# Attention in eight batches: six of seven products of y in blocks, seeded by copies within PSUM, with sums moved behind the last product and x1 added early

## The chip, the cores and the metric

The kernel runs on one core of a Trainium2 chip. A core has five engines, each with its own queue worked off in order: TensorE (PE in the profile; its weight loads are PEld), VectorE (DVE), ScalarE (ACT), GpSimd (POOL) and SyncE (SP, which only issues DMAs here). Engines wait for each other through semaphores. Matmul results go to PSUM, eight banks of 512 floats for each of 128 partitions; everything else lies in SBUF. The metric is device time in microseconds (us), as the median of three runs.

## The reference: what is computed

For each of 8 batches, with x1 (here `x`) and x2 (here `ctx_2048`) of 512 channels by 1024 positions, all in float32:

```python
q = jnp.einsum('bcn,dc->bnd', x1, Wq) + bq
k = jnp.einsum('bcn,dc->bdn', x2, Wk) + bk[:, None]
v = jnp.einsum('bcn,dc->bdn', x2, Wv) + bv[:, None]
attn = jax.nn.softmax(jnp.einsum('bnd,bdm->bnm', q, k), axis=2)
attn_out = jnp.einsum('bcm,bnm->bcn', v, attn)
return attn_out + x1
```

q and k have 64 rows. The kernel takes the value product in another order: first y = x2 times the transposed exponentials (512 x 1024 x 1024 per batch), divided by the sums of the exponentials, then Wv times y (512 x 512 x 1024), plus bv and x1.

## The kernel before, in words

Both large products are done by the Winograd form of Strassen's scheme: each matrix is cut into 2 x 2 blocks, and seven products of block sums take the place of eight. `MULT` names them 1, 2, 6, 7, 5, 3, 4, with a left and a right factor each: a11, a12, a21, a22 and the sums S1 to S4 on the left (x2, transposed, loaded as four blocks), t11 to t22 and T1 to T4 on the right (exponentials). Products 1, 6, 5, 3 add up in the two PSUM banks called a (a0, a1, one for each 128 rows of a block), products 2, 7, 4 in the banks c. A running sum is a state: ACT copies it out to SBUF (u1, u6, u5) where a later result needs it. The first stage gives the blocks y11, y12, y21, y22, the second (`second`) the output blocks in the same manner, with w in place of a and y in place of t.

A product of the first stage has two forms. The full one (`multiply`, L321) is 8 matmuls of 512 columns, two instructions each. The one in blocks applies the scheme once more inside (`inner_left`, `inner_right` make the sums on DVE, L355 and L367; `inner_product`, L374, the 7 small products, 14 matmuls of 256 columns, two instructions each). Its seven partial results pass through a bank called chain and one called third, both from the pool `sc`, which also serves the scores; ACT copies the chain's states to a tile d (L383), and DVE adds d afterwards (`complete`, L452, and the lines that follow: L462, L471, L483). `multiply_2` does the same for product 2 in a form of its own (L418).

The loop is over batches: `period(s, n, nn, nnn)` is written for batch s while the scores, maxima and exponentials of the next batch n and the queries and keys of the one after it (nn) are slipped in between. All orders are written by hand; each engine does its part of the program in the order of the text, and a waiting instruction holds up all that stand behind it on its engine. A column half h of a batch (0 or 1, 512 positions) has tiles e[h]; its scores are four pairs of matmuls, the third pair in a bank pair of the first stage (c for half 0, a for half 1), the others in `sc`. DVE takes maxima over the tiles (L211, L215), POOL an all-reduce over partitions (L221), DVE subtracts the maximum (L249), ACT takes the exponential (L253). Sums of exponentials go the same way (L226), by DVE for half 1 (`sums`), and for half 0 by accumulating DMAs of POOL (`add_tile`, L555). `shares` inverts them: a DMA gathers the row into 128 partitions, DVE inverts, and two DMAs through DRAM spread it again.

Which products are in blocks depends on the batch: products 3 and 4 in batch 0; 2, 3 and 4 in batches 1 and 6; 2, 7, 3 and 4 in batches 2 to 5 and 7 (`seven`). S1, S2, S3 of the next batch are DVE sums at the end of a period (`sum_a`, L110), S4 one behind product 2, T4 from batch 2 on a copy by ACT and an accumulating DMA (L278, L280). `evict_y` adds and scales the blocks of y (L502, L505, L507). `evict_o` adds the bias (L548 on DVE, L544 on ACT), lets POOL add x1 from DRAM by an accumulating DMA (L551) and SP store (L552). q lies twice in SBUF, at both halves of the partitions; ACT issues the two DMAs that double it (L167).

Of the kernel before, what the change touches and what calls it, by code (L numbers as in the profile page):

```python
# [15 lines left out]
def kernel(  # L16
# [48 lines left out]
    P = 128  # L65
# [35 lines left out]
    def left_sums(a, *ks):  # L101

        for k in ks:
            x, y, op = {
                "S1": ("21", "22", ALU.add),
                "S2": ("11", "S1", ALU.subtract),
                "S3": ("11", "21", ALU.subtract),
                "S4": ("12", "S2", ALU.add),
            }[k]
            nc.vector.tensor_tensor(a["21" if k == "S3" else k], a[x], a[y], op)  # L110
            if k == "S3":
                a["S3"] = a["21"]

    class Batch:
        def __init__(self, b):
            self.b = b
            self.a, self.e, self.t, self.y, self.o = {}, {}, {}, {}, {}
            self.mx, self.top, self.den, self.few, self.rden = {}, {}, {}, {}, {}
            self.tmp, self.bank = {}, {}
            self.inner = {}  # L120
# [19 lines left out]

    def project(s, nm, w_sb, bank=None):
# [16 lines left out]
    def queries(s):  # L158

        ps = project(s, "q", wq_sb)  # L160
        s.q = sb.tile([P, N], F32, tag="q", name=f"q_{s.b}", bufs=2)
        for h, r, o in ((0, lo, hi), (1, hi, lo)):
            nc.scalar.activation(
                s.q[r, ts(h, H)], ps[r, :], AF.Identity, bias=bq_sb[r, :]
            )
        for h, r, o in ((0, lo, hi), (1, hi, lo)):
            nc.scalar.dma_start(s.q[o, ts(h, H)], s.q[r, ts(h, H)])  # L167
# [64 lines left out]
    def shares(s, h):  # L232

        nc.vector.reciprocal(s.few[h], s.few[h])
        row = dram.tile([1, H], F32, tag="row", name=f"row_{s.b}_{h}")
        nc.gpsimd.dma_start(row.rearrange("o (p f) -> (o p) f", p=P), s.few[h])
        s.rden[h] = s.den[h]
        nc.gpsimd.dma_start(s.rden[h], row.broadcast_to([P, H]))
# [32 lines left out]
    def sum_t4(s):  # L271

        s.t["T4"] = t4 = sb.tile([P, MH, H], F32, tag="eT4", name=f"eT4_{s.b}")
        if s.b < 2:
# [7 lines left out]
    def sum_e(s, *ks):  # L282
        for i in (0, 2):
# [4 lines left out]
    def sum_y(s, k):  # L288
        if k == "T1":
            for n in ("T1", "T2", "T4"):  # L290
                s.y[n] = sb.tile([P, 2, H], F32, tag=f"y{n}", name=f"y{n}_{s.b}")
            s.y["T3"] = s.y["12"]
        right_sums(s.y, k)
# [14 lines left out]
    def multiply(s, stage, i, left, right, n_k, last=False, hook=None):  # L308
# [3 lines left out]
        ka, kb, bank, opens = MULT[i]  # L312
        for j in range(2):
# [21 lines left out]

    LEFT = (
        ("S1", "21", "22", ALU.add),
        ("S2", "11", "S1", ALU.subtract),
        ("S3", "11", "21", ALU.subtract),
        ("S4", "12", "S2", ALU.add),  # L340
    )
    RIGHT = (
        ("T1", "12", "11", ALU.subtract),
        ("T2", "T1", "22", ALU.subtract),
        ("T3", "22", "12", ALU.subtract),
        ("T4", "21", "T2", ALU.add),
    )

# [9 lines left out]
    def inner_right(s, i, x, *tags):  # L358
# [4 lines left out]
        shape = [P, 4 // len(tags), MH // 2, H // 2]  # L363
        sums = [sb.tile(shape, F32, tag=t, name=f"eI{i}{t}_{s.b}") for t in tags]
        for z, (k, x, y, op) in enumerate(RIGHT):
            v[k] = sums[z // shape[1]][:, z % shape[1]]
            nc.vector.tensor_tensor(v[k], v[x], v[y], op)  # L367
        s.inner[i, "t"] = v
# [16 lines left out]
    def inner_bank(s, i, z):  # L385
        return ps_s.tile([P, 2, H], F32, tag="sc", name=f"ps_i{i}{z}_{s.b}")[:, 0, left]

    def multiply_2(s):

        chain = ps_a.tile([P, H // 2], F32, tag="c0", name=f"ps_i20_{s.b}")  # L390
        second = ps_a.tile([P, H // 2], F32, tag="c1", name=f"ps_i21_{s.b}")
        third = inner_bank(s, 2, 2)
        uv = sb.tile([P, 4, H // 2], F32, tag="i2", name=f"i2_{s.b}")
        u, v = uv[:, 0:2], uv[:, 2:4]
        for z, ps, opens, *copies in (
            (1, chain, True, v[:, 0, :]),
            (2, second, True),
            (6, chain, False, u[:, 0, :]),
            (7, third, True, v[:, 1, :]),
            (5, chain, False, u[:, 1, :]),  # L400
            (4, third, False),
            (3, chain, False),
        ):
            inner_product(s, 2, z, ps, opens, *copies)

        def evict():

            u0, u1 = s.tmp[1][:, 0, :], s.tmp[1][:, 1, :]
            s.y["11"] = y = sb.tile([P, 2, H], F32, tag="y11", name=f"y11_{s.b}")
            for out, x, z in (  # L410
                (u0[:, left], u0[:, left], v[:, 0, :]),
                (y[:, 0, left], second, u0[:, left]),
                (u1, u1, u.rearrange("p a n -> p (a n)")),
                (y[:, 1, right], v[:, 1, :], u1[:, right]),
                (y[:, 1, left], third, u1[:, left]),
                (y[:, 0, right], chain, u0[:, right]),
            ):
                nc.vector.tensor_tensor(out, x, z, ALU.add)  # L418

        return evict  # L420

    def multiply_onto(s, i, d_tag, v_tag, hooks={}):
# [5 lines left out]
        bank, opens = MULT[i][2:]  # L428
        if opens:
            for j in range(2):  # L430
                s.bank[bank, j] = ps_a.tile([P, H], F32, tag=f"{bank}{j}", name=f"ps_y{bank}{j}_{s.b}_{i}")
        b0, b1 = (s.bank[bank, j] for j in range(2))
        chain, third = inner_bank(s, i, 0), inner_bank(s, i, 2)
# [503 lines left out]
```

## Time and profile before

| what | value |
|---|---|
| median of 3 runs | 691.22 us (691.01 to 691.45) |
| span of the profiled execution | 689.5 us |
| its own time | not listed apart from the three runs |
| granted TensorE clock over the span | 0.999 |
| batch 3, from the start of its product 1 to that of the next batch | 83.66 us |
| DMA moved | 109.05 MB, mean 158 GB/s |

The profile records one execution. A group of it has the kernel's line, the engine, the operation, what is written from what, and how often; then the busy time, the mean of one, and the idle time of the engine ahead of it with what ended it. Instructions of one engine overlap a little at their ends, so two in a row take less than the sum of their durations. Batches are told apart by the order of time: a period begins with product 1 of the first stage (8 matmuls into ps_ya from e and a).

### The profile page before, as it was taken

What the parts mean: (1) busy time and instruction counts of PE and PEld (TensorE: products, weight loads), DVE (VectorE), ACT (ScalarE), POOL (GpSimd) and SP (SyncE); (2) the same over time, 40 slices, a digit from 0 to 9 for tenths busy, and PEclk for the clock granted to TensorE, in tenths of its full rate; (3) what the DMA queues carried; (4) which work ended last, traced back from release to release, by engine and by line L of the source; (5) the groups of instructions that cost most, each with busy time, mean ns of one, the idle gap of its engine ahead of it and who ended that gap; (6) DMA issues with size and microseconds to landing.
All of it is one profiled execution on the core that took longest, in us unless ns stands there. A gap on an engine that the chain in (4) does not pass through costs nothing.

```text
span 689.5 us, 6656 instructions
## 1 busy us (share of the span) xinstructions
PE 683.1 (99%) x2252; PEld 365.3 (53%) x2252; DVE 630.4 (91%) x809; ACT 275.7 (40%) x439; POOL 189.3 (27%) x147
## 2 busy tenths in 40 slices
PE   9999999999999999999999999999999999999997
PEld 5333554535545465455654566454754545545763
DVE  1999999988999889998999989999899988999894
ACT  2734263146233562435533454324544245333220
POOL 0124113521423123231232321423223241324100
PEclk9999999999999999999999999999999999999999
DMA  9666266954558854696638867298642874259403
GB/s 301 263 218 231 70 183 120 252 162 92 184 106 208 236 100 160 129 243 182 125 130 160 241 176 166 69 187 224 181 81 41 185 200 77 62 108 248 102 0 123
DMA packets 44723, 109.05 MB, mean 158 GB/s; under 512 B 4880, under 2 KB 7184, under 8 KB 44688
## 3 DMA queue, kind: packets, MB, share of 16 engines
q0 software_dynamic: 17424, 36.25, 30.1%
q1 hardware_dynamic: 25856, 70.13, 29.4%
q10 hardware_dynamic: 1408, 2.23, 1.1%
q8 instruction: 18, 0.29, 0.2%
q14 instruction: 17, 0.14, 0.1%
HBM read 72.62 MB, written 16.81 MB: 130 GB/s over the span
## 4 chain that ended last, share of the span: by engine, by line
PE 94%; DMA 3%; SPq 1%; ACT 1%; DVE 1%; issue 0%; DVEq 0%
PE ps_ya L321 24%; PE ps_i L374 17%; PE ps_oa L321 16%; PE ps_oc L321 12%; PE ps_s L191 6%; PE ps_yc L374 5%; PE ps_q L149 4%; PE ps_k L149 3%; PE ps_ya L374 3%; PE ps_yc L321 3%; DMA a<-in_x2T_dram 1%; DMA x_in_x_dram<-in_x_dram 1%; DMA x_head<-in_x_dram 1%; PE ps_sc L191 1%; PE ps_sa L191 1%; DVE aS L110 0%
## 5 line engine op out<-in xcount | busy, mean ns | idle before, releaser
L321 PE MATMUL ps_ya<-eT,aS 128*128 128x512 f32 x256 | 113.1, 595 | 0.0
L332 ACT COPY uy<-ps_ya 128x512 f32<-128x512 f32 x48 | 28.0, 586 | 138.9 <-PE ps_ya L321 124.9
L321 PEld LDWEIGHTS ps_ya<-eT,aS 128*128 128x128 f32 x256 | 48.0, 190 | 60.9 <-issue 58.8
L253 ACT ACTIVATE e<-e 128x1024 f32<-128x1024 f32 x60 | 63.0, 1059 | 42.3 <-DVE e L249 40.8
L249 DVE TENSOR_TENSOR e<-e,top 128x1024 f32<-128x1024 f32 x60 | 69.8, 1214 | 11.0 <-POOL top L221 11.0
L221 POOL PARTITION_ALL_REDUCE top<-max x16 | 32.8, 2052 | 154.6 <-DVE max L215 79.3
L226 POOL PARTITION_ALL_REDUCE den<-sum x16 | 59.2, 3701 | 40.8 <-DVE sum L215 35.8
L321 PE MATMUL ps_oa<-yT,w_S 128*128 128x512 f32 x128 | 57.6, 593 | 0.0
L321 PE MATMUL ps_oc<-y,w 128*128 128x512 f32 x128 | 57.6, 593 | 0.0
L321 PE MATMUL ps_ya<-e,a 128*128 128x512 f32 x128 | 56.3, 593 | 0.3 <-ACT e L244 0.3
L200 ACT COPY e<-ps_s 128x1024 f32<-128x1024 f32 x46 | 45.7, 1028 | 19.3 <-PE ps_s L191 18.1
L332 ACT COPY uo<-ps_oa 128x512 f32<-128x512 f32 x48 | 27.4, 583 | 53.0 <-PE ps_oa L321 41.3
L383 ACT COPY d<-ps_i 128x256 f32<-128x256 f32 x84 | 29.3, 374 | 47.6 <-PE ps_i L374 47.0
L551 POOL DMA_DIRECT2D uo<-in_x_dram x21 | 24.9, 1184 | 85.0 <-DVE uo L548 85.0
L191 PE MATMUL ps_s<-q,k 64*128 64x512 f32 x188 | 47.3, 608 | 0.8 <-ACT q L590 0.8
L555 POOL DMA_DIRECT2D sum<-e x21 | 25.7, 1222 | 66.5 <-DMA sum<-e 32.7
L321 PEld LDWEIGHTS ps_ya<-e,a 128*128 128x128 f32 x128 | 24.2, 190 | 31.3 <-issue 29.6
L321 PEld LDWEIGHTS ps_oa<-yT,w_S 128*128 128x128 f32 x128 | 24.2, 190 | 30.8 <-issue 29.9
L321 PEld LDWEIGHTS ps_oc<-y,w 128*128 128x128 f32 x128 | 24.0, 190 | 31.0 <-issue 28.5
L211 DVE TENSOR_TENSOR max<-max,e 128x1024 f32<-128x1024 f32 x30 | 36.7, 1225 | 3.0
L507 DVE TENSOR_TENSOR y<-y,den 128x512 f32<-128x512 f32 x54 | 33.7, 681 | 0.0
L548 DVE SCALAR_TENSOR_TENSOR uo<-ps_oc,bv_sb,uo 128x512 f32<-128x512 f32 x42 | 29.5, 741 | 1.6 <-PE ps_oc L321 1.6
(142 smaller groups left out, 1274.5 us busy)
## 6 DMA issues: line engine op xcount, KB each, us to landing
x_in_x_dram<-in_x_dram SPq DMA_DIRECT2D x60, 512.0 KB, 6.2
a<-in_x2T_dram SPq DMA_DIRECT2D x32, 512.0 KB, 6.3
sum<-e POOLq DMA_DIRECT2D x21, 512.0 KB, 5.1
uo<-in_x_dram POOLq DMA_DIRECT2D x21, 512.0 KB, 6.4
out_dram<-uo SPq DMA_DIRECT2D x21, 512.0 KB, 4.1
eT<-eT POOLq DMA_DIRECT2D x12, 512.0 KB, 6.8
den<-row POOLq DMA_DIRECT2D x16, 256.0 KB, 3.6
r<-in_x_dram POOLq DMA_DIRECT2D x7, 512.0 KB, 8.7
```

The costliest lines, as they stand in the source:

```text
L149: nc.tensor.matmul(ps[r, :], w_sb[:, c, :], s.x[:, c, ts(h, H)], start=(c == 0), stop=(c == CT - 1),)
L191: nc.tensor.matmul(ps[g], s.k[r, ts(i, P)], s.q[r, ts(h, H)], start=True, stop=True)
L200: nc.scalar.copy(e[:, :, i, :], whole)
L211: nc.vector.tensor_tensor(f, e[:, :, 0, :] if i == 1 else f, e[:, :, i, :], op)
L221: nc.gpsimd.partition_all_reduce(s.top[h], s.mx[h][:, 0, :], P, ReduceOp.max)
L226: nc.gpsimd.partition_all_reduce(s.den[h], s.mx[h][:, 0, :], P, ReduceOp.add)
L249: nc.vector.tensor_tensor(e, e, top, ALU.subtract)
L253: nc.scalar.activation(e, e, AF.Exp)
L321: nc.tensor.matmul(ps[:, n], left[ka][:, k, ts(j, P)], right[kb][:, k, n], start=opens and k == 0, stop=i in (2, 3, 4) and k == n_k - 1, s ...
L332: nc.scalar.copy(s.tmp[i][:, j, :], ps)
L374: nc.tensor.matmul(ps, s.inner[i][ka][:, k, :], s.inner[i, "t"][kb][:, k, :], start=opens and k == 0, stop=z in (2, 3, 4) and k == MH // 2 ...
L507: nc.vector.tensor_tensor(y[:, j, :], y[:, j, :], rden, ALU.mult)
```

## The change

In batches 1 to 7 (the second batch on) products 1 and 2, 7, 3 and 4 are in blocks, and in batches 1 to 5 product 5 as well; 6 stays full. Batch 0 keeps 3 and 4.

`multiply_seeded` takes the place of the block form for 1, 2, 7 and 3. Its two result banks are new, and are begun not by a matmul but by ACT copies of the chain's states, from one PSUM bank into another; the small products 2, 4 and 3 then add onto what was copied. DVE's `complete` adds the one remaining piece v into the second bank, in place. Products 5 and 4 keep the tile d. Product 3 no longer adds onto the state of bank a: with signs turned in S4 and in the sums of w, y22 - y12 comes out directly as T3 (`evict_t3`), and y12 is never made. Product 7's banks are copied out for it by ACT (`copy_7`).

Work that moves: S1 of the next batch is loaded and summed by two DMAs (`begin_s1`, `end_s1`), S2 and S3 are made by an ACT negation and an accumulating DMA (`negate`, `add_11`), T3 of the first stage likewise (`sum_t3`; by DVE in batches 0 and 7), T4 by copy and DMA from batch 1 on. The total of half 0's exponentials is joined behind the last output product of the period before, its inverse and the spreading of it stand apart (`invert`, `spread`). Right-hand sums T1 and T3 are one instruction. The scaling of y11, T3 and y22 is one instruction each, behind the scores of half 1. The second stage's product 1 opens two banks of `sc` (p), is copied by ACT into bank a, and product 2 adds onto p; block 11's output then goes by ACT. x1 is added to block 21's state ahead of its last product (`add_x1`). The DMAs that double q are issued by SP; the queries of a batch use bank c0, and are taken out in the middle of product 5 (`evict_q`).

The core of the diff, helpers first:

```diff
+            if k == "S3":
+                nc.vector.tensor_tensor(a["21"], a["11"], a["21"], ALU.subtract)
+                a["S3"] = a["21"]
+            elif k == "S4":
+                nc.vector.scalar_tensor_tensor(a[k], a["12"], -1.0, a["S2"], ALU.mult, ALU.subtract)
+            else:
+                x, y, op = {"S1": ("21", "22", ALU.add), "S2": ("11", "S1", ALU.subtract)}[k]
+                nc.vector.tensor_tensor(a[k], a[x], a[y], op)
...
+    def begin_s1(s):
+        s.a["S1"] = sb.tile([P, MH, C // 2], F32, tag="aS1", name=f"aS1_{s.b}")
+        nc.sync.dma_start(s.a["S1"], x2T[s.b, 1, 0])
+    def end_s1(s):
+        nc.gpsimd.dma_start(s.a["S1"], x2T[s.b, 1, 1], accum_op=ALU.add)
+    def negate(s, k):
+        if k == "S2":
+            s.a[k] = sb.tile([P, MH, C // 2], F32, tag="aS2", name=f"aS2_{s.b}")
+        else:
+            s.a[k] = s.a["21"]
+        nc.scalar.mul(s.a[k], s.a["S1" if k == "S2" else "21"], -1.0)
+    def add_11(s, k):
+        nc.gpsimd.dma_start(s.a[k], x2T[s.b, 0, 0], accum_op=ALU.add)
...
-    def queries(s):
-        ps = project(s, "q", wq_sb)
+    def queries(s, bank=None):
+        ps = project(s, "q", wq_sb, bank)
         s.q = sb.tile([P, N], F32, tag="q", name=f"q_{s.b}", bufs=2)
-        for h, r, o in ((0, lo, hi), (1, hi, lo)):
-            nc.scalar.activation(
-                s.q[r, ts(h, H)], ps[r, :], AF.Identity, bias=bq_sb[r, :]
-            )
-        for h, r, o in ((0, lo, hi), (1, hi, lo)):
-            nc.scalar.dma_start(s.q[o, ts(h, H)], s.q[r, ts(h, H)])
+        def evict():
+            halves = ((0, lo, hi), (1, hi, lo))
+            for h, r, o in halves:
+                nc.scalar.activation(
+                    s.q[r, ts(h, H)], ps[r, :], AF.Identity, bias=bq_sb[r, :]
+                )
+            for h, r, o in halves:
+                nc.sync.dma_start(s.q[o, ts(h, H)], s.q[r, ts(h, H)])
+        return evict
...
+    def sum_t3(s, i):
+        t3 = s.t["T3"][:, i : i + 2, :]
+        nc.scalar.mul(t3, t3, -1.0)
+        nc.gpsimd.dma_start(t3, s.t["22"][:, i : i + 2, :], accum_op=ALU.add)
+    def copy_u1(s, j):
+        if j == 0:
+            s.tmp[1] = sb.tile([P, 2, H], F32, tag="u1", name=f"uy1_{s.b}")
+        nc.scalar.copy(s.tmp[1][:, j, :], s.bank["a", j])
...
-        if k == "T1":
+        y = s.y
+        if k == "T2":
             for n in ("T1", "T2", "T4"):
-                s.y[n] = sb.tile([P, 2, H], F32, tag=f"y{n}", name=f"y{n}_{s.b}")
-            s.y["T3"] = s.y["12"]
-        right_sums(s.y, k)
+                y[n] = sb.tile([P, 2, H], F32, tag=f"y{n}", name=f"y{n}_{s.b}")
+            nc.vector.tensor_tensor(y["T2"], y["11"], y["T3"], ALU.add)
+        else:
+            nc.vector.tensor_tensor(y[k], y["22" if k == "T1" else "21"], y["T2"], ALU.subtract)
...
+    def multiply_o1(s):
+        for j in range(2):
+            s.bank["p", j] = ps = ps_s.tile([P, 2, H], F32, tag="sc", name=f"ps_o1{j}_{s.b}")[:, 0, :]
+            for k in range(2):
+                nc.tensor.matmul(
+                    ps, w["11"][:, k, ts(j, P)], s.y["11"][:, k, :], start=k == 0, stop=False, skip_group_check=True
+                )
+            s.bank["a", j] = a = ps_a.tile([P, H], F32, tag=f"a{j}", name=f"ps_oa{j}_{s.b}_1")
+            nc.scalar.copy(a, ps)
...
+        both, t2, t4 = sums[0][:, 0:2], sums[-1][:, last - 2], sums[-1][:, last - 1]
+        part = x.rearrange("p (q k) (r n) -> p q k r n", q=2, r=2)
+        nc.vector.tensor_tensor(
+            both, part[:, :, :, 1, :], part[:, 0].rearrange("p k r n -> p r k n"), ALU.subtract
+        )
+        nc.vector.tensor_tensor(t2, both[:, 0], v["22"], ALU.subtract)
+        nc.vector.tensor_tensor(t4, v["21"], t2, ALU.add)
+        s.inner[i, "t"] = v | {"T1": both[:, 0], "T3": both[:, 1], "T2": t2, "T4": t4}
...
+    def multiply_seeded(s, i, v_tag, hooks={}):
+        bank = MULT[i][2]
+        b0, b1 = (
+            ps_a.tile([P, H], F32, tag=f"{bank}{j}", name=f"ps_y{bank}{j}_{s.b}_{i}") for j in range(2)
+        )
+        s.bank[bank, 0], s.bank[bank, 1] = b0, b1
+        chain, third = inner_parts(s, i)
+        v = sb.tile([P, 2, H], F32, tag=v_tag, name=f"v{i}_{s.b}")[:, 0, left]
+        for z, ps, opens, out, of in (
+            (1, chain, True, b0[:, left], chain),
+            (7, third, True, v, third),
+            (6, chain, False, b1[:, left], chain),
+            (2, b0[:, left], False, None, None),
+            (5, chain, False, b0[:, right], chain),
+            (4, b1[:, left], False, b1[:, right], chain),
+            (3, b0[:, right], False, None, None),
+        ):
+            inner_product(s, i, z, ps, opens)
+            if out is not None:
+                nc.scalar.copy(out, of)
+            if z in hooks:
+                hooks[z]()
+        def complete():
+            b = b1.rearrange("p (a n) -> p a n", a=2)
+            nc.vector.tensor_tensor(b, b, v.unsqueeze(1).to_broadcast([P, 2, H // 2]), ALU.add)
+        return complete
...
+    def multiply_5(s, hooks):
+        d, complete = multiply_onto(s, 5, "u5", "r", hooks)
         complete()
         for j in range(2):
+            nc.vector.tensor_tensor(d[:, j, :], s.bank["a", j], d[:, j, :], ALU.add)
+        s.tmp[5] = d
+    def copy_7(s, j):
+        if j == 0:
+            s.tmp[7] = sb.tile([P, 2, H], F32, tag="u1", name=f"uy7_{s.b}")
+        nc.scalar.copy(s.tmp[7][:, j, :], s.bank["c", j])
+    def evict_t3(s):
+        s.y["T3"] = y = sb.tile([P, 2, H], F32, tag="y12", name=f"yT3_{s.b}")
+        for j in range(2):
+            nc.vector.tensor_tensor(y[:, j, :], s.bank["a", j], s.tmp[7][:, j, :], ALU.add)
+    def scale_y(s, *ks):
+        for k in ks:
+            rden = s.rden[k in ("T3", "22")].unsqueeze(1).to_broadcast([P, 2, H])
+            nc.vector.tensor_tensor(s.y[k], s.y[k], rden, ALU.mult)
...
+    def add_x1(s, k):
+        nc.gpsimd.dma_start(s.tmp[RESULT[k][1]], block(s, k, x1), accum_op=ALU.add)
```

The body of `period` for batches 1 to 7, as it stands after (what is for batch 0 alone is left out):

```python
else:
    complete_1 = multiply_seeded(s, 1, "y11")
    sum_e(s, "T1", "T2")
    complete_1()
    for i in range(1, MH):
        fold(s, 1, i, "sum", ALU.add)
    total(s, 1)
    invert(s, 0)
    complete_2 = multiply_seeded(
        s, 2, "y22", {5: lambda: copy_u1(s, 0), 4: lambda: copy_u1(s, 1)}
    )
    if n:
        sum_t3(s, 0)
        sum_t3(s, 2)
    complete_2()
    evict_y(s, "11")
    if n is None:
        sum_e(s, "T3")
    sum_t4(s)
    first(6)
    inner_left(s, 7, s.a["S3"], "yT4")
    if five:
        inner_left(s, 5, s.a["S1"], "i2")
        inner_right(s, 5, s.t["T1"], "y21", "u1")
    sum_a(s, "S4")
    if n:
        evict_q = scores_0()
    spread(s, 0)
    shares(s, 1)
    inner_right(s, 7, s.t["T3"], "yT1", "yT2")
    inner_left(s, 3, s.a["S4"], "aI3")
    if five:
        multiply_5(s, {6: evict_q})
    else:
        first(5)
    inner_right(s, 3, s.t["22"], "eT1")
    if n:
        lower(n, 0, 0)
    complete_7 = multiply_seeded(s, 7, "y12")
    complete_7()
    evict_y(s, "22")
    if n:
        for i in range(1, MH):
            lower(n, 0, i)
    else:
        inner_left(s, 4, s.a["22"], "a12")
        inner_right(s, 4, s.t["T4"], "eT2")
    hooks = {7: lambda: copy_7(s, 0), 2: lambda: copy_7(s, 1)}
    if n:
        hooks |= {6: lambda: exponential(n, 0, 0), 4: lambda: exponential(n, 0, 1)}
    complete_3 = multiply_seeded(s, 3, "r", hooks)
    complete_3()
    evict_t3(s)
if n:
    if s.b:
        load_a(n, "11")
    begin_s1(n)
    scores_and(n, 1, 2, "a", nothing)
...
    else:
        copy_first(n, 0)
        add_tile(n, 0, 1)
    end_s1(n)
    if nn:
        next_keys()
if late and n:
    inner_left(s, 4, s.a["22"], "a12")
    inner_right(s, 4, s.t["T4"], "eT2")
if late:
    scale_y(s, "11", "T3", "22")
sum_y(s, "T2")
sum_y(s, "T1")
...
hooks = {}
...
elif n:
    hooks = {6: lambda: add_exponential(2), 5: lambda: exponential(n, 0, 3)}
multiply_4(s, hooks)
if late and n:
    negate(n, "S3")
if n:
    load_a(n, "12")
if nn:
    load_a(nn, "21", "22")
evict_y(s, "21")
scale_y(s, "21")
sum_y(s, "T4")
if late and n:
    for i in range(1, MH):
        fold(n, 1, i, "max", ALU.max)
    highest(n, 1)
    add_tile(n, 0, 3)
    add_11(n, "S3")
second(1)
...
second(6)
if n:
    add_x1(s, "21")
...
second(2)
evict_o(s, "11")
if n:
...
    inner_left(n, 1, n.a["11"], "i2")
second(5)
if n:
    for i in range(2 if s.b == 0 else 0, MH):
        exponentials(n, 1, i)
second(7)
if n:
    negate(n, "S2")
    add_11(n, "S2")
evict_o(s, "22")
if n:
    inner_right(n, 1, n.e[0][:, 0], "yT1", "yT2")
    inner_left(n, 2, n.a["12"], "aS4")
    inner_right(n, 2, n.e[0][:, 1], "eT4")
    second(3)
    evict_o(s, "12")
    second(4)
    total(n, 0)
    evict_o(s, "21")
...
```

## The prediction

> **What bounds the kernel now.** The page's first part comes first, to see which engine has no room, then its chain of work, to see whether that engine sets the end.
>
> ```profile
> PE 683.1 (99%) x2252; PEld 365.3 (53%) x2252; DVE 630.4 (91%) x809; ACT 275.7 (40%) x439; POOL 189.3 (27%) x147
> ...
> PE 94%; DMA 3%; SPq 1%; ACT 1%; DVE 1%; issue 0%; DVEq 0%
> ```
>
> TensorE (PE) never rests, and 94% of the chain is its matmuls; its work is the time. But VectorE (DVE) is at 91%, so the next question is how close it comes inside one batch. The windows view, cut at batch starts (busy columns PE, PEld, DVE, ACT, POOL), for batch 3 and batch 6:
>
> ```profile
> 288.16:371.82 83.66, 83.66 (x281) 45.74 (x281) 80.06 (x105) 35.64 (x57) 24.72 (x19) 1.00 0.67 166
> ...
> 539.15:617.00 77.85, 77.56 (x238) 41.43 (x237) 72.87 (x91) 31.72 (x49) 24.72 (x19) 1.00 0.53 122
> ```
>
> PE has no gap at all, the clock is whole, and DVE keeps only 3.6 us of idle in 83.66. A shorter PE period is therefore worth something only down to DVE's own length. The chain in order of time prices a product of PE in both forms:
>
> ```profile
> 288.16 6.87 PE ps_ya L321 x16
> 295.02 6.04 PE ps_i L374 x28
> ```
>
> A full product (L321) is 6.87 us, one in blocks (L374) 6.04. Last, where DVE and PE meet: the scores of half 1 write bank a as their third tile, which is free when DVE has read product 3 out of it (L483); and block 22's output (L548) cannot start on DVE before PE's output product 7. From the timeline, all engines:
>
> ```profile
> 334.09 1.29 DVE L483 TENSOR_TENSOR y<-ps_ya,d 128x512 f32<-128x512 f32 x2
> ...
> 336.05 0.60 PE L191 MATMUL ps_sa<-q,k 64*128 64x512 f32 x2
> ```
>
> DVE is 0.7 us early there. That is the margin to watch.
>
> **PE: what goes.** Products by blocks per batch, before: 2, 3, 4, 4, 4, 4, 3, 4 (batches 0 to 7). After: 2, then 6 in batches 1 to 5 (1, 2, 5, 7, 3, 4), 5 in batches 6 and 7. That is 14 more, each 6.87 - 6.04 = 0.83 us: **-11.6 us**, all of it on the chain. A middle batch falls from 83.66 to 82.0, batch 1 from 84.47 to 82.0 (three products). The second stage keeps its matmuls: `multiply_o1` opens two other banks, and the copies that pass product 1 on are as many as the two it replaces.
>
> **ACT.** A seeded product has five 128x256 copies (372 ns rows at L383), as the older block form did. Per middle batch the new ones are about 10 such copies for products 1 and 5 (3.7 us) less two 586 ns copies, `copy_7` (1.2), the two negations of T3 (2.1), those of S2 and S3 (2.1), and block 11's output (1.4): 36 to 45 us of 82. No trace row has a PSUM-to-PSUM copy; the nearest, PSUM to SBUF, is 0.37, and a 512-wide one, 0.58, bounds it above: 0.2 more a copy, hidden unless in product 3. There ACT must fit, between its third input's matmuls and the last (3.45 us), three seed copies (1.1), two `copy_7` (1.2) and one exponential (1.06): 3.3 us. Cover nearly gone; I take 0.1 us a batch.
>
> **DVE: the segment that decides.** I price it start to start from the timeline of 288 to 372 us, since instructions overlap at their ends: 1.14 us for 128x1024 (1.25 if the next reads its result), 0.60 (0.72) for 512, 0.34 (0.45) for 256, 0.66 for the 512 with a scalar. By these the old segment, from block 22's output (one period before 366.44) to the end of L483 (335.29), is 49.9 with one stretched S4, plus waits of 1.83 and 0.49 = 52.2; measured 52.5. So the method holds to 0.3.
>
> The new segment: outputs of 22 and 21 2.6; five right-hand sums (1, 2, 5, 7, 3) at 2.53 = 12.65 (the joined T1/T3 instruction saves nothing: 1.25 + 0.72 + 0.60 against 2.53 read off); four left-hand sums at 1.58 = 6.3 (1.46 read off, and one more dependent pair); T1 and T2 4.8; exponential sums with two half-folds and reciprocals 5.15; maxima 4.5; S4 1.25; five completions 3.1; four two-part evictions (11, u5, 22, T3) 4.9; four subtractions of the maximum 4.55. Sum **49.8**. It gained products 1 and 5 (about 11) and lost T3, the S1-S3 sums, adding product 7 to two states, and the six-part eviction of 11.
>
> Then POOL's all-reduces, which stretch DVE. The timeline of DVE and of POOL:
>
> ```profile
> 134.99 0.42 DVE L418 TENSOR_TENSOR y<-ps_i,uy 128x256 f32<-128x256 f32 x1
> 135.33 2.20 DVE L418 TENSOR_TENSOR uy<-uy,i 128x512 f32<-128x512 f32 x1
> ...
> 302.36 3.73 DVE L110 TENSOR_TENSOR aS<-a,aS 128x1024 f32<-128x1024 f32 x1
> ```
> ```profile
> 134.66 3.32 POOL L226 PARTITION_ALL_REDUCE den<-sum  x1 [1.27 <-DVE sum L215]
> ...
> 302.82 3.18 POOL L226 PARTITION_ALL_REDUCE den<-sum  x1
> ```
>
> S4 took 3.73 instead of 1.2 and ended with the reduce: 2.45 lost. The instruction from PSUM at 134.99 kept its 0.42, the next, two SBUF inputs, took 2.20 instead of 0.68. Now two sum reduces lie in the segment (half 0's was elsewhere) and one of the maximum (excess 0.8 in the row at 349.02). Ends: 0, and 2 x 2.45 + 0.8 = 5.7. I take 3.4: half 0's reduce runs first beside block 21's output and catches T1 about 1.2 us in (1.6 lost); half 1's runs beside the completion of 2 and the eviction of 11, both from PSUM, for its first 1.9 us (1.0 lost); the maximum 0.8. 53.2 in all.
>
> The Trainium skill, "GPSIMD Engine Reference", section Specifications, says that GpSimd shares its SBUF interfaces with VectorE and contends with VectorE instructions that have two SBUF inputs. These rows agree; by that rule alone the second loss is the 1.0 above, by the S4 row alone 2.45, and the time 7 us longer. It speaks against this change, which puts another reduce among such instructions.
>
> The loop closes through PE: third tile of scores (336.05) to the end of output product 7 (364.8) is 28.75 us, unchanged. 28.75 + 53.2 + 0.25 for two handovers (estimate from 0.1 to 0.15 us gaps in the timeline) = 82.2, against PE's 82.0. Stall 0.2, with ACT's 0.1: 0.3 in batches 1 to 5, **+1.5 us**. Batch 6 lacks product 5 by blocks (5.9 us of DVE) and only 3.6 us of queries, batch 7 all of the next batch's work: no stall there. After the scores DVE has slack of about 1.3 us before output product 7.
>
> **Waits and queues.** The q halves are doubled by SP instead of ACT. In batches 0 to 5 this stands behind the x2 load; in the head before it, so SP waits for both activations and issues 1.2 us of copies before the four loads. The timeline there:
>
> ```profile
> 37.26 1.99 SPq L126 DMA_DIRECT2D x_in_x_dram<-in_x_dram  x4
> 37.27 1.39 ACT L163 ACTIVATE q<-ps_q,bqk_sb 64x512 f32<-64x512 f32 x2 [2.57 <-PE ps_q L149]
> ...
> 47.10 0.20 PEld L149 LDWEIGHTS ps_k<-x_in_x_dram,wqk_sb 128*64 128x64 f32 x4 [0.97 <-DMA x_in_x_dram<-in_x_dram]
> ```
>
> PE already waits for the last chunk, so a load 2.0 us later (39.3 for 37.26) is 2.0 on the chain at most, 0 if the load shortens; I take **+1.9**.
>
> POOL issues five more accumulating DMAs per batch (T3 twice, S1, S2, S3): 1.1 us each, 5.5 on an engine with 57 us free. Queue 0 used 30.1% of the DMA engines for 36.25 MB; 18 MB more is 15%, 61% to 77% in all. T3's pair is issued about 20 us into the batch, behind half 1's reduce, lands (6.8 us, the T4 row) near 28, and DVE wants it at 29: 1 us of cover, and a late one enters the loop whole. S2 and S3 have over 10 us; block 21's x1, issued near 72, has 4 before its output; load of S1 on SP stands behind a11 only. Freed early is the u6 state, whose store was a 13.9 us wait of ACT, off the chain.
>
> **Sum.** -11.6 + 1.9 + 1.5 = -8.2. The profiled span 689.5 becomes 681.3; its own time isn't listed apart, the runs' median lies 1.7 above the span: **683.0**.
>
> **Rivals.**
> - Clean (0.17): DVE's holds are 2 us or less, the loop stays under 82.0: -11.6 + 1.9 = 681.5, or 679.6 if the head costs nothing. For it: one-SBUF-input row. Against: 91% busy DVE.
> - DVE becomes the bound (0.16): both sum reduces cost 2.45, the segment is 55.5, the loop 84.5, stall 2.5 a batch: -11.6 + 1.9 + 12.5 = +2.8, **694.0**, slower. It decides from a segment of 54.9, 1.7 above mine. For: S4's row. Against: instructions from PSUM stand beside half 1's reduce.
> - T3 comes late (0.08): with DMA at 77% the pair takes 10 us: 2.2 us into each of five loops, 11 more than mine: 694. For: 8.7 us landings of r. Against: T3 is ahead of T4 in its queue.
> - The block form doesn't shorten PE (0.04): seeds reach the banks late and each of 14 products waits 0.8: 691 to 694. Against: L374 products with copies in between run at 6.04 now.
>
> **The numbers.** Main case 0.55, its own range 680.8 to 688. Of the last three, two thirds of 0.16 and half of 0.08 and 0.04 end slower, 0.17 together; of the 0.11 left, 0.04 lies within 0.2% (1.4 us, about what a measurement of this kernel can tell from no change) and 0.07 is faster: with main and clean 0.79. The range 679.5 to 692 leaves out about 0.13 of the 694 cases above, and a little below.
>
> **What would show it.** Right: middle batches of 82.0 to 82.5, products at 6.04 in fourteen more places, PE's wait before bank a's scores of a few tenths, the last keys chunk at 49. Wrong: that wait near 2 us in every batch, DVE with no idle between bank a and block 22's output, or DVE waiting for T3's DMA before product 7's right-hand sums.

## The result and the profile after

The changed kernel takes 689.07 us (median of 18 runs, 687.92 to 691.51), the kernel before 690.99 beside it (18 runs, 690.60 to 692.02): a ratio of 0.9977, 95% interval 0.9969 to 0.9985. It is faster by 1.9 us where 8.2 were forecast. The profiled execution has a span of 688.0 and took 690.05.

The first and fourth part of the page of after (busy time of each engine; shares of the chain that ended last, where "issue" is time in which an engine waited for nothing that the profile shows):

```profile
PE 674.7 (98%) x2420; PEld 399.0 (58%) x2420; DVE 614.7 (89%) x763; ACT 336.5 (49%) x564; POOL 218.5 (32%) x182
...
PE 70%; DMA 15%; DVE 6%; issue 5%; ACT 2%; POOL 2%; SPq 0%; DVEq 0%; POOLq 0%; ACTq 0%
```

PE's work did shrink, by 8.4 us busy, and DVE's by 15.7. But DMA, 3% of the chain before, is now 15%, and PE's share fell from 94% to 70%. The time is no longer PE's alone: something waits for transfers.

Where, the windows view tells, cut at the first matmul of product 1 (window, its length, busy PE, PEld, DVE, ACT, POOL, clock, DMA share, GB/s). Batches 1 to 6 of after:

```profile
119.75:203.45 83.70, 82.66 (x305) 50.79 (x304) 77.71 (x99) 44.01 (x74) 28.95 (x24) 1.00 0.87 211
203.45:285.44 81.99, 81.99 (x305) 50.56 (x304) 77.80 (x99) 43.73 (x74) 29.10 (x24) 1.00 0.83 207
285.44:367.43 81.99, 81.99 (x305) 50.55 (x304) 77.80 (x99) 43.74 (x74) 29.08 (x24) 1.00 0.84 209
367.43:449.90 82.47, 82.27 (x306) 50.48 (x305) 77.99 (x99) 43.74 (x74) 29.15 (x24) 1.00 0.79 197
449.90:537.68 87.78, 83.95 (x305) 51.06 (x304) 76.89 (x99) 43.84 (x74) 28.97 (x24) 0.98 0.79 182
537.68:614.23 76.55, 76.18 (x262) 46.09 (x260) 70.73 (x88) 41.45 (x68) 28.90 (x24) 1.00 0.67 147
```

Batches 2 and 3 are what the products alone make: 81.99, PE without a gap. From before's lengths less 0.83 for each new product in blocks, batch 1 should be 82.0, 4 and 5 82.0, 6 76.2 and 7 71.7. They are 1.7, 0.5, 5.8, 0.35 and 2.1 longer (batch 7 runs from 614.23 to 688.0, 73.77): 10.4 of the 11.6 us that the products saved. Batch 5 alone holds more than half.

PE's waits of after (what it waited for: us in all, times, longest), and PE's timeline at the places in batches 4 and 5 (start, us; in brackets the idle time ahead; the first row is the beginning of product 6, x5 of 16):

```profile
PE ps_ya L380 <- ACT uy L335: 5.6, 3, 3.8
PE ps_i3chain L442 <- ACT ps_ya L479: 1.0, 1, 1.0
```
```profile
379.89 2.41 PE L380 MATMUL ps_ya<-eT,aS 128*128 128x512 f32 x5 [0.20 <-ACT uy L335]
...
461.12 1.02 PE L442 MATMUL ps_yc<-e,aI 128*128 128x256 f32 x4
465.97 8.83 PE L380 MATMUL ps_ya<-eT,aS 128*128 128x512 f32 x16 [3.83 <-ACT uy L335]
```

Product 6 adds onto bank a, and must wait until ACT's `copy_u1` (L335) has copied product 1 out. In batch 5 that is 3.83 us late, and product 6 then takes 8.83 instead of 7.03: 5.6 of the batch's 5.8 us. What ACT waits for, by its waits:

```profile
ACT uy L335 <- DMA out_dram<-r: 8.0, 4, 4.5
```

`out_dram<-r` is the store of an output block. `evict_o` (L605) puts block 11's output into a tile with the tag u1, the buffer that `copy_u1` of the next batch wants. So the copy waits until the block of the batch before has had x1 added by POOL's DMA and has been stored. The chain in order of time shows how long that takes (the first row is block 11's store ahead of batch 4's copy, the others lead to batch 5's):

```profile
369.04 10.13 DMA out_dram<-r
...
430.96 6.28 DMA sum<-e
437.25 4.41 issue
...
443.73 12.15 DMA r<-in_x_dram
...
455.94 9.32 DMA out_dram<-r
...
465.34 0.59 ACT uy L335
```

x1 needs 12.15 us to land, and the store 9.32. Neither is special to batch 5. For the seven batches that are followed by another, block 11's x1 takes 11.4 to 12.2 us from issue to landing and its store 8.7 to 10.5; before, they took 5.6 to 5.9 and 2.8 to 4.1. So even in a regular period the store lands about 11 us into the next batch (in batch 3 at 296.6, 11.2 into it), just where `copy_u1` comes: ACT waits there 0.3 us in batch 3, 0.9 in batch 4, 4.5 in batch 5 and 2.3 in batch 7. What made batch 5 so late is seen on POOL. Its timeline, first for the period before batch 3, then for that before batch 5:

```profile
262.34 1.19 POOL L619 DMA_DIRECT2D sum<-e  x1 [5.90 <-ACT e L297]
...
273.39 1.20 POOL L619 DMA_DIRECT2D sum<-e  x1 [0.60 <-issue]
274.13 1.39 POOL L171 DMA_DIRECT2D a<-in_x2T_dram  x1
275.01 1.74 POOL L565 DMA_DIRECT2D uo<-in_x_dram  x1
275.73 2.26 POOL L615 DMA_DIRECT2D r<-in_x_dram  x1
...
419.73 1.23 POOL L619 DMA_DIRECT2D sum<-e  x1 [13.04 <-issue]
...
430.96 1.19 POOL L619 DMA_DIRECT2D sum<-e  x1 [9.07 <-ACT ps_oa L404]
...
441.67 1.20 POOL L619 DMA_DIRECT2D sum<-e  x1 [4.42 <-ACT e L297]
442.40 1.39 POOL L171 DMA_DIRECT2D a<-in_x2T_dram  x1
442.97 2.04 POOL L565 DMA_DIRECT2D uo<-in_x_dram  x1
443.73 2.50 POOL L615 DMA_DIRECT2D r<-in_x_dram  x1
```

Two things add up here. First, in every period block 11's x1 is the fourth of four accumulating transfers issued within some 2.3 us: half 0's sum tile 3 (`sum<-e`), S3 (`a`), block 21's x1 (`uo`), then it (`r`). Secondly, tile 3 may only be added once tile 2 has landed. Tile 2 (262.34 and 430.96) takes about as long in both periods, 10.5 and 10.2 us from issue to landing. But in batch 4 it goes out 63.5 us after the batch's start, in batch 2 after 58.9, because tile 1 (419.73) went out 1.5 us later there and took 10.7 us to land instead of 7.5. Half a us after tile 2's landing tile 3 follows, 69.9 us into batch 2 and 74.2 into batch 4, and all that stands behind it on POOL is 4 us late with it. (The row at 441.67 names an exponential of ACT as what ended POOL's wait; tile 3's own exponential ran at 424.87 already. The chain counts tile 2's transfer only to 437.25, where POOL's reduce ended, and calls the rest "issue".)

The transfers of after as the page has them (KB each, median us to landing; queue 0 carries POOL's):

```profile
q0 software_dynamic: 22464, 54.60, 44.0%
...
uo<-in_x_dram POOLq DMA_DIRECT2D x14, 512.0 KB, 10.3
r<-in_x_dram POOLq DMA_DIRECT2D x14, 512.0 KB, 12.3
```

54.60 MB in 44.0% of 688.0 us is 0.180 MB/us, 2.9 us for each 512 KB. The row of four before batch 5 agrees with this estimate: its first landed 5.5 us after its issue, the others 3.0, 3.2 and 2.5 us after one another. The medians of the page mix blocks: uo is x1 of blocks 21 and 22, r that of 11 and 12.

Batch 1 has another loss: DVE, on its timeline, waits at the start for half 0's total, runs late, and passes it on through ACT's copy to product 3's chain (the 1.0 in PE's waits).

```profile
123.81 0.69 DVE L252 TENSOR_TENSOR sum<-sum 128x512 f32<-128x512 f32 x1 [3.13 <-DMA sum<-e]
```

### The profile page after: what moved, and what is told of

Same layout as the page of the kernel before. It is cut to its first block, busy times and chain, and to the rows that moved or that the text cites. A ratio compares the mean times of both kernels' runs of the same rounds, so it can differ in the third digit from the quotient of the medians.

```text
span 688.0 us, 7199 instructions
## 1 busy us (share of the span) xinstructions
PE 674.7 (98%) x2420; PEld 399.0 (58%) x2420; DVE 614.7 (89%) x763; ACT 336.5 (49%) x564; POOL 218.5 (32%) x182
## 3 DMA queue, kind: packets, MB, share of 16 engines
q0 software_dynamic: 22464, 54.60, 44.0%
## 4 chain that ended last, share of the span: by engine, by line
PE 70%; DMA 15%; DVE 6%; issue 5%; ACT 2%; POOL 2%; SPq 0%; DVEq 0%; POOLq 0%; ACTq 0%
PE ps_ya L380 11%; PE ps_yc L442 6%; PE ps_oa L380 6%; PE ps_ya L442 6%; PE ps_s L228 5%; DMA r<-in_x_dram 5%; DMA out_dram<-r 4%; DMA sum<-e 4%; PE ps_oc L380 4%; PE ps_k L181 3%; PE ps_q L181 3%; PE ps_i4chain L442 3%; PE ps_o L400 3%; PE ps_i3chain L442 3%; PE ps_i7chain L442 2%
## 5 line engine op out<-in xcount | busy, mean ns | idle before, releaser
L380 PE MATMUL ps_ya<-eT,aS 128*128 128x512 f32 x176 | 79.5, 606 | 5.6 <-ACT uy L335 5.6
L293 DVE TENSOR_TENSOR e<-e,top 128x1024 f32<-128x1024 f32 x60 | 69.9, 1218 | 0.0
L380 PEld LDWEIGHTS ps_ya<-eT,aS 128*128 128x128 f32 x176 | 33.6, 193 | 47.8 <-issue 38.7
L380 PE MATMUL ps_oc<-yT,w 128*128 128x512 f32 x128 | 57.4, 592 | 0.0
L380 PEld LDWEIGHTS ps_oc<-yT,w 128*128 128x128 f32 x128 | 24.3, 190 | 30.6 <-issue 28.9
L391 ACT COPY uy<-ps_ya 128x512 f32<-128x512 f32 x24 | 13.9, 589 | 39.1 <-PE ps_ya L380 36.8
L228 PEld LDWEIGHTS ps_s<-q,k 64*128 64x128 f32 x188 | 17.0, 186 | 24.5 <-issue 17.5
L479 ACT COPY ps_ya<-ps_i1chain 128x256 f32<-128x256 f32 x28 | 10.0, 357 | 42.2 <-PE ps_i1chain L442 38.7
L547 DVE TENSOR_TENSOR y<-y,den 128x1024 f32<-128x1024 f32 x24 | 29.3, 1221 | 0.3
L418 DVE TENSOR_TENSOR aI<-a 128x256 f32<-128x256 f32 x58 | 29.0, 541 | 0.0
L380 PE MATMUL ps_oa<-y,w_S 128*128 128x512 f32 (+1 forms) x68 | 28.8, 567 | 0.0
L400 PE MATMUL ps_o<-y,w 128*128 128x512 f32 x64 | 28.8, 592 | 0.0
```

The lines of the kernel that those rows point to most:

```text
L228: nc.tensor.matmul(ps[g], s.k[r, ts(i, P)], s.q[r, ts(h, H)], start=True, stop=True)
L293: nc.vector.tensor_tensor(e, e, top, ALU.subtract)
L380: nc.tensor.matmul(ps[:, n], left[ka][:, k, ts(j, P)], right[kb][:, k, n], start=opens and k == 0, stop=i in (2, 3, 4) and k == n_k - 1, s ...
L391: nc.scalar.copy(s.tmp[i][:, j, :], ps)
L400: nc.tensor.matmul(ps, w["11"][:, k, ts(j, P)], s.y["11"][:, k, :], start=k == 0, stop=False, skip_group_check=True)
```

## The experiments

Theory A: the loss is mostly the store of block 11, which stands late behind POOL's queue and holds the u1 buffer. Theory B: it is the DMA load as such, or DVE near its bound, and the u1 wait is only where it shows.

**1. Block 11's output in another buffer**, that of product 3's left sums (aI3), free at the time. Nothing else is moved.

```diff
-            o = sb.tile([P, 2, H], F32, tag="u1" if k == "11" else "r", name=f"r{k}_{s.b}")
+            o = sb.tile([P, 2, H], F32, tag="aI3" if k == "11" else "r", name=f"r{k}_{s.b}")
```

> Block 11's output gets the buffer of aI3 (free from product 3 to the next batch's left sums of 3) instead of u1; nothing else changes. Theory A, the late store of block 11 holds ACT's copy of u1 and with it product 6: the waits at that copy go (0.2, 3.8 and 1.6 us in batches 4, 5 and 7 of the changed kernel), and the slow matmuls behind them (1.8 us in batch 5), about 8 us in all: 681 to 683 us, middle batches all at 82.0. Theory B, the DMA engines are simply too loaded (share 0.79 to 0.84 in batches 2 to 5): another transfer comes late in the same places, at least 5 of the 8 us stay: 686 to 689.

Measured: 682.17 us (682.04 to 682.81), ratio 0.9874 (0.9861 to 0.9888); span 680.0, 8.0 under the changed kernel's. The windows view of this kernel, batches 1 and 5:

```profile
119.46:203.15 83.69, 82.65 (x306) 50.76 (x305) 77.70 (x99) 44.01 (x74) 29.07 (x24) 1.00 0.86 211
...
449.12:531.13 82.01, 82.01 (x306) 50.47 (x305) 76.40 (x99) 43.78 (x74) 28.98 (x24) 1.00 0.85 195
```

Batch 5 is 82.01 instead of 87.78, batch 7 72.32 instead of 73.77, and the wait at L335 is gone. x1 of block 11 still lands in 12.2 us and its store starts as late as before (6.2 us into batch 5); it only holds nothing up that is wanted. So A: it is the shared buffer, not the load. Batch 1 keeps its 1.7.

**2. Tile 3's addition issued behind block 11's x1**, with u1 shared as in the change. This tells whether the queue's order makes the store late.

```diff
             highest(n, 1)
-            add_tile(n, 0, 3)
             add_11(n, "S3")
...
         if n:
-            if s.b == 0:
-                add_tile(n, 0, 3)
+            add_tile(n, 0, 3)
             inner_left(n, 1, n.a["11"], "i2")
```

> In batches 1 to 6 the adding of tile 3 to half 0's sums is issued behind block 11's x1 instead of ahead of S3 and both x1. Same transfers, same tiles, another order on POOL's queue. Theory A with the queue as its source (POOL waits up to 4.4 us there for the tile before, and everything behind it starts late): block 11 leaves 1 to 5 us earlier, most of the 8 us come back, less what DVE waits for the later total of half 0 (0 to 2 us a batch): 682 to 687. Theory B: same load, 687 to 690.

Measured: 681.73 us (680.98 to 682.32), ratio 0.9865 (0.9852 to 0.9879). POOL's timeline of this kernel at the place, and SP's, with the store of block 11:

```profile
437.16 2.08 POOL L615 DMA_DIRECT2D r<-in_x_dram  x1
440.67 1.18 POOL L619 DMA_DIRECT2D sum<-e  x1 [1.43 <-DMA sum<-e]
```
```profile
447.80 0.40 SPq L616 DMA_DIRECT2D out_dram<-r  x1
```

Batch 5 starts at 448.66 here; the store begins 0.9 us before it instead of 6.0 behind the start, and batch 5 is 81.99. The store itself still takes 10.1 us. So the order of the queue, which sets when the store starts, is shown as the source of the lateness. It costs DVE something: tile 3 now lands in 9.6 to 12.6 us, and DVE waits for half 0's total seven times, 6.6 us in all, none of which reaches PE in batches 2 to 5.

**3. The opposite: block 11's x1 and its store issued behind block 22's**, u1 shared.

```diff
                 nc.scalar.activation(o[:, j, :], s.bank[bank, j], AF.Identity, bias=bias(j))
+            if k == "11":
+                s.o[k] = o
+                return
...
         if n:
+            nc.gpsimd.dma_start(s.o["11"], block(s, "11", x1), accum_op=ALU.add)
+            nc.sync.dma_start(block(s, "11", out), s.o["11"])
             inner_right(n, 1, n.e[0][:, 0], "yT1", "yT2")
```

> Block 11's x1 and store are issued behind block 22's output, some 5 us later. Theory A: every batch from 2 on waits 3 to 7 us at the copy of u1, and its matmuls then run slowly for some us: 705 to 735 us. Theory B: the order doesn't matter at equal load: 687 to 692.

Measured: 705.74 us (704.39 to 707.30), ratio 1.0214 (1.0200 to 1.0229), the low end of A's range. PE's waits, and two answers of its timeline, for batches 3 and 4 of this kernel:

```profile
PE ps_ya L380 <- ACT uy L335: 15.8, 7, 4.4
```
```profile
304.35 7.13 PE L380 MATMUL ps_ya<-eT,aS 128*128 128x512 f32 x16 [1.42 <-ACT uy L335]
...
388.58 8.83 PE L380 MATMUL ps_ya<-eT,aS 128*128 128x512 f32 x16 [1.97 <-ACT uy L335]
```

Now all seven batches, 1 to 7, wait at L335. It also gives a row of idle times and what follows them, taken up below.

**4. T3 made by DVE instead of POOL's two DMAs**, on top of experiment 1. It takes 12 transfers (6.3 MB) off the queue, and puts about 2 us a batch on DVE (busy 79.9 in a middle batch instead of 77.8): B and the forecast's loop of DVE and PE part here.

```diff
-            if n:
-                sum_t3(s, 0)
-                sum_t3(s, 2)
             complete_2()
             evict_y(s, "11")
-            if n is None:
-                sum_e(s, "T3")
+            sum_e(s, "T3")
```

> As e1_own11, and T3 of the first stage by DVE in all batches instead of by ACT and two accumulating DMAs. DVE's segment from output product 7 to bank a grows by 2.3 us; in batch 3 of the changed kernel it had 1.6 us of waits. If the loop of the prediction holds, PE stalls 0.5 to 1.2 us ahead of the scores' third tile in batches 1 to 5: 3 to 6 us slower than e1_own11, 684 to 688. If the DMA load is what counts (theory B), 12 fewer transfers of 512 KB make it faster than e1_own11 by 1 us or more.

Measured: 687.15 us (686.74 to 687.92), ratio 0.9943 (0.9930 to 0.9957): 5.0 us slower than experiment 1, with less traffic. Middle batches are 82.74 (PE's starts 206.20, 288.94, 371.69, 454.43, 537.17), batch 1 85.86. So the load in itself isn't the limit, and DVE is close to one: some 2 us more of it lengthen every middle batch by 0.75. On PE's timeline 0.47 of this arise inside product 3, where ACT's seed copy into bank a comes late, and the rest ahead of the scores' third tile.

**5. The q halves doubled by ACT**, as before the change, on top of experiment 1.

```diff
-                nc.sync.dma_start(s.q[o, ts(h, H)], s.q[r, ts(h, H)])
+                nc.scalar.dma_start(s.q[o, ts(h, H)], s.q[r, ts(h, H)])
```

> As e1_own11 (682.2 us), with the DMAs that double q issued by ACT again, as in the kernel before. By the prediction's step the head should gain 1.9 us: 680 to 681. By the trace of the changed kernel, where the last keys chunk landed at the same time as before although its load was issued 1.9 us later, nothing: 682 to 682.5; in the middle of product 5 ACT spends no time that shows on issuing two DMAs.

Measured: 682.18 us (681.95 to 682.39), ratio 0.9870 (0.9856 to 0.9885): no difference to experiment 1's 682.17. Who issues the two DMAs costs nothing that can be seen here.

**6. Half 0's sums begun earlier in batch 0**, on top of experiment 1: the first copy behind the scores of half 1, tile 1 inside product 4, tile 2 behind it, tile 3 behind output product 1. So that POOL is free for them, its all-reduce of half 1's maxima moves behind product 4. It is to take batch 1's wait for the total.

```diff
-            else:
-                copy_first(n, 0)
+            copy_first(n, 0)
+            if s.b:
                 add_tile(n, 0, 1)
...
-            highest(n, 1)
+            fold_halves(n, 1, ALU.max)
...
-            hooks = {6: lambda: exponential(n, 0, 1), 5: lambda: exponential(n, 0, 2)}
+            hooks = {6: lambda: add_exponential(1), 5: lambda: exponential(n, 0, 2)}
...
+        if s.b == 0:
+            highest(n, 1, halves=False)
+            add_tile(n, 0, 2)
...
-            copy_first(n, 0)
             exponential(n, 0, 3)
-            add_tile(n, 0, 1)
-            add_tile(n, 0, 2)
+            add_tile(n, 0, 3)
...
-            if s.b == 0:
-                add_tile(n, 0, 3)
```

> As e1_own11, and in batch 0 the sums of batch 1's exponentials over half 0 begin earlier: first copy at the scores of half 1, tiles 1 and 2 added around product 4, tile 3 behind output product 1. Batch 1 of e1_own11 takes 83.7 us where the next take 82.0, and DVE waits 3.1 us for the last of these additions at its beginning. If that wait is the cause (DVE late, so ACT's copy of product 7's bank late, so product 3's seed late), 1.7 us go: 680.3 to 681. If batch 1 is slow for another reason, 682.

Measured: 680.38 us (679.73 to 680.72), ratio 0.9843 (0.9829 to 0.9858). DVE's timeline and the windows view of this kernel:

```profile
120.35 0.68 DVE L252 TENSOR_TENSOR sum<-sum 128x512 f32<-128x512 f32 x1
```
```profile
119.52:201.51 81.99, 81.99 (x306) 50.52 (x305) 77.81 (x99) 43.87 (x74) 29.06 (x24) 1.00 0.84 210
```

The total is joined 3.1 us sooner than in experiment 1 (123.50) and batch 1 is 81.99: its 1.7 us came from that wait.

**7. Experiments 6 and 2 together**: tile 3 late from batch 1 on.

```diff
             highest(n, 1)
-            add_tile(n, 0, 3)
             add_11(n, "S3")
...
         if n:
+            if s.b:
+                add_tile(n, 0, 3)
             inner_left(n, 1, n.a["11"], "i2")
```

> As e6_own11_sum0, with tile 3 of half 0's sums behind block 11's x1 in batches 1 to 6, as in e2_tile3_late. With block 11 in a buffer of its own the order should no longer matter: within 0.5 us of e6_own11_sum0; if e2's order had a value of its own (682.2 against 681.7), 680 to 680.5.

Measured: 680.29 us (679.68 to 680.62), ratio 0.9842 (0.9827 to 0.9857), the same as 6. Once the buffer is its own, the queue's order is worth nothing. These two are the fastest, 10.6 and 10.7 us under the kernel before.

**8. Product 5 full in all batches**, on top of experiment 1. Are the products in blocks worth their DVE work?

```diff
-        five = late and nn is not None
+        five = False
```

> As e1_own11, with product 5 full in every batch, and the queries taken out at once. PE gains five times 0.83 us of work, 4.15; DVE loses 6 us of work a batch. If blocks are worth their PE time: 686.3, or 684.6 if DVE's slack also removes batch 1's 1.7 us. If blocks cost something elsewhere (copies, sums), less than 4 us slower than e1_own11: 682 to 684.

Measured: 684.31 us (683.69 to 685.41), ratio 0.9904 (0.9888 to 0.9921). Every one of batches 1 to 5 is 82.82 (starts 119.40, 202.22, 285.04, 367.86, 450.69, 533.51), 0.83 over 81.99; batch 1 has no loss either, where DVE has 6.1 us less to do (busy 71.6 instead of 77.7). 5 x 0.83 less batch 1's 1.7 is 2.4, and the difference to experiment 1 is 2.1. So product 5 in blocks is worth its 0.83 in batches 2 to 5, and in batch 1 the wait for the total took back as much as two such products.

## Why the prediction was wrong, and where it was right

| term | forecast, us | measured, us |
|---|---|---|
| 14 products in blocks | -11.6 | -11.6 |
| head: x2 loads behind q's copies | +1.9 | 0 (all up to batch 1's start: 119.75 for 120.03, -0.3) |
| DVE and ACT stalls, batches 1 to 5 | +1.5 | +1.7, all in batch 1, of another kind |
| wait for block 11's store | none | +7.7 (0.5 + 5.8 + 1.45, what experiment 1 took away in batches 4, 5, 7) |
| batches 6 and 7, the rest | 0 | +1.0 (0.35 and 0.65, cause open) |
| sum | -8.2 | -1.5 (spans: 688.0 - 689.5) |

**The step that failed** is "Waits and queues". It counted POOL's new accumulating DMAs by their issue time ("5.5 on an engine with 57 us free") and their share of the DMA engines, gave the new ones and block 21's x1 a cover each, and put the path of an old one that now stands behind them at nothing, without a reason: block 11's x1, its store, the buffer u1, `copy_u1`, product 6. It named the buffer that the change frees (u6, whose store had already made ACT wait 13.9 us before) without asking which one block 11's output goes into. In its place the runs showed a wait worth 7.7 us, which a buffer of its own takes away (experiment 1). (Block 21's x1, given 4 us of cover, was late once, by 2.0 us on DVE.)

Half of this could be had from the page before. Queue 0 moved 36.25 MB in 30.1% of 689.5 us, 0.175 MB/us, so about 3 us for each 512 KB and some 12 for the fourth in a row, as an estimate. Block 11's x1, issued next to block 21's (near 72 us into the period in the forecast, 72.3 in batch 2's trace), so lands 2 us into the next batch. With the 7.2 us that the page before has for stores of r, its store ends near 9, and `copy_u1` comes near 11: 2 us of cover, which the sum should have named and priced. The other half that page does not show: the store takes 8.7 to 10.5 us, which leaves no cover in any batch, and in one period the whole row goes out 4 us late.

The rival "T3 comes late" named the right kind of mechanism, a transfer late behind others, at the wrong transfer: in the trace after DVE has no wait for T3. It is luck that the measured time lies between 679.5 and 692: the upper part of that range stood for a late T3 and for DVE as the bound. Experiment 1, without the wait, is 8.7 us under the kernel before, near the 8.2 of the forecast, but this too is partly luck: the head's 1.9 did not come, and the 1.7 and 1.0 that did had other causes.

**PE.** Right to the hundredth: the batches without a wait are 81.99 where 82.0 stood, products in blocks keep 6.04, and the copies within PSUM cost 357 ns where the forecast's nearest row, from PSUM to SBUF, had 370 (L479, x28, in the page).

**The DVE segment.** Forecast 53.2 including holds of 3.4, loop 82.2. Measured in batch 3, from the output of block 22 (277.70) to the end of T3's eviction (331.55), 53.85, of which 1.6 are DVE's own waits for ACT: 52.25. The holds by POOL's reduces were smaller. DVE's timeline and POOL's, after:

```profile
288.20 2.18 DVE L306 TENSOR_TENSOR eT<-e,e 128x1024 f32<-128x1024 f32 x1
...
300.79 1.17 DVE L418 TENSOR_TENSOR aI<-a 128x256 f32<-128x256 f32 x2
...
313.94 1.41 DVE L434 TENSOR_TENSOR eI7yT<-eI7yT,e 128x512 f32<-128x512 f32 x1
```
```profile
287.07 3.23 POOL L263 PARTITION_ALL_REDUCE den<-sum  x1 [2.69 <-DVE sum L252]
...
299.11 3.22 POOL L263 PARTITION_ALL_REDUCE den<-sum  x1 [7.92 <-DVE few L271]
...
312.81 2.75 POOL L258 PARTITION_ALL_REDUCE top<-max  x1 [5.54 <-DVE few L271]
```

They cost 0.96, 0.41 and 0.72 over the usual 1.22, 0.76 and 0.69: 2.1 where 3.4 stood (1.6, 1.0, 0.8). Each fell near where the forecast had it. PE never waited before bank a's scores in batches 2 to 5, so the 0.3 a batch was 0, and "clean" was the better case for DVE. Experiment 4 shows that the loop itself was no illusion: some 2 us more of DVE, and every middle batch is 0.75 longer, though more of it through product 3 and ACT's copies than at bank a's scores, where the forecast looked.

**Batch 1.** Its 1.7 us are near the sum forecast for all stalls, by chance: PE loses most of them in product 3, whose seed from ACT comes late behind DVE. The wait for half 0's total there was not foreseen: in batch 0 the tiles' additions stand late, and the join behind the last product finds the third not yet landed.

**The head.** The load did start 2.0 us later, but PE's wait for its last chunk was as before. SP's timeline and PE's, after:

```profile
39.23 1.84 SPq L137 DMA_DIRECT2D x_in_x_dram<-in_x_dram  x4
```
```profile
47.09 1.08 PE L181 MATMUL ps_k<-x_in_x_dram,wqk_sb 128*64 128x512 f32 x4 [0.23 <-DMA x_in_x_dram<-in_x_dram]
```

The last chunk was used at 47.09, before at 47.10. The forecast had both ends, 2.0 and 0, and chose the wrong one: the load took 6.4 us instead of 8.5.

**What stays open.** Why tile 1 goes out later in batch 4 and takes 10.7 us (7.5 in batches 2 and 3) is only argued: SP's four x loads go out at 419.83 there, 0.1 us behind tile 1's issue, and share the DMA engines. It isn't chance, since tile 1 goes out 51.8 us into batch 4 in experiments 1 and 2 as well, for 50.8 in batches 2 and 3 after. Why the store of block 11 takes three times as long as before is not tested either; while it is under way, from 455 to 466, the DMA engines' share is 1.02, and three more accumulations of POOL's queue are still to land. The late store may also explain why the changed kernel's runs scatter over 3.6 us, and experiment 1's over 0.8: the fastest of the 18 runs has a mean granted clock of 1.000, the two slowest 0.995. But four runs are few, and one execution of each kernel was traced.

## What to carry to other kernels

When a change adds transfers to a queue, estimate the landing of every transfer behind them, old ones too, from the queue's own rate (bytes over share times span, here 0.175 to 0.18 MB/us, 3 us per 512 KB), and follow each, through its store, to the buffer that it keeps occupied: who takes the same tag next, and when. An average (57 us free on POOL, 75% of the DMA engines) says nothing on seven transfers issued within 10 us. Look at each batch by itself: two at exactly the predicted time beside one that is 5.8 us longer pointed here to a single wait whose cover was used up, not to an engine that is too full.

## What the runs showed of the hardware that was not expected

**In these runs a PE pause of about 2 us cost as much again.** The windows view of after, around the wait of 3.83 us (the clock is the last figure but two):

```profile
455.00:466.00 11.00, 7.17 (x35) 5.97 (x33) 9.62 (x10) 2.46 (x7) 1.89 (x2) 1.00 1.02 241
466.00:470.00 4.00, 4.00 (x6) 1.66 (x7) 3.70 (x9) 4.00 (x6) 3.70 (x5) 0.64 0.67 241
470.00:475.00 5.00, 5.00 (x13) 2.13 (x13) 4.86 (x8) 1.23 (x3) 2.87 (x4) 0.94 0.91 166
475.00:480.00 5.00, 5.00 (x24) 1.82 (x24) 1.87 (x3) 4.25 (x6) 0.00 (x0) 1.00 1.07 209
```

The granted clock is 0.64 over the 4 us after the wait, 0.94 over the next 5, and whole from 475 on. In windows of 1 us it is still whole until 467, 0.50 from 468 to 470 and whole again from 471: here the drop comes behind the pause, while PE works. Experiment 3 gives a series for product 6 (idle ahead of it, then its length): 0.87, 1.10 and 1.42 us are followed by 7.13; 1.97 and 2.95 by 8.83; 4.38 by 9.37. In batch 7, where products 6 and 5 follow each other, the changed kernel and experiment 3 have (PE's timelines; the second row ends with its window):

```profile
628.05 14.00 PE L380 MATMUL ps_ya<-eT,aS 128*128 128x512 f32 x32 [1.57 <-ACT uy L335]
...
642.47 8.07 PE L380 MATMUL ps_ya<-eT,aS 128*128 128x512 f32 x11 [3.14 <-ACT uy L335]
```

After 1.57 us of idle the 32 matmuls take 14.00, as long as without a wait (13.9 to 14.3 in experiments 1, 2 and 6); after 3.14 they take 17.08 in all. So in these nine gaps the price of a wait jumps between 1.57 and 1.97 us of idle, by 1.7 to 3 us. Whether the limit is a fixed length, so few gaps don't show. The Trainium skill, "TensorE: Matmul & The Clock Gate", section "HAM oscillation — how this bites in real kernels", puts the limit for gaps of an idle PE at about 3.4 us; these rows have it lower, since a gap of 1.97 already slowed the next product.

**The backlog is felt on another queue too, and medians hide it.** With the added accumulations, SP's plain loads of `a` land in 9.8 us instead of 6.3 (medians), though SP's own queue got only the load for S1 and q's two copies more in a period; its loads of x hardly changed (6.9 for 6.2). The stores of r seem faster, 6.2 for 7.2. But after they are those of block 11 (8.7 to 10.5) and block 12 (2.9 to 3.6) in one median, and before those of block 12 alone, while block 11's store, then one of `uo`, took 2.8 to 4.1. Read one by one, the store that the kernel waits for became three times as long.
